# A transformer block with routed experts on one core: the setup's order of work on VectorE, and the Newton step of an inverse root

## The chip, the cores and the metric

The kernel runs on one core of a Trainium2 chip, as one program from the load of the inputs to the store of the output. The metric is device time in microseconds (us), lower is better. Three timed runs of the kernel before gave 1874.04, 1875.34 and 1876.84, a median of 1875.34.

A core has five engines that run side by side, each with its own stream of instructions in order: TensorE (PE, matrix products and transposes; the loads of its stationary operand are listed apart as PEld), VectorE (DVE), ScalarE (ACT), GpSimd (POOL) and SyncE (SP, which here issues DMAs). ACT and POOL can issue DMAs too. Engines wait for each other by semaphores.

## What is computed

The input x has 8 sequences of 1024 rows of 128 numbers, float32. Two layers are added to it: attention with relative positions, then a mixture of 8 experts with 2 chosen for each row. Cut to what matters:

```python
x = x + attn(layernorm(x), ...)          # 8 heads of 16; attn has a layernorm of its own inside
x = x + ffn(layernorm(x), ...)           # router, top 2 of 8 experts, each 128 -> 2 x 512 -> 128

# attn
xn = (inputs - mu) / sqrt(var + 1e-05) * ln_gamma + ln_beta
q, k, v = xh @ Wq + bq, xh @ Wk + bk, xh @ Wv + bv
score = (einsum(q + u_bias, k) + rel_shift(einsum(q + v_bias, p))) / sqrt(e)
ctx = softmax(score) @ v;  return ctx @ Wo + bo

# ffn: router, then sum over chosen experts of weight * (x1 * gelu(x2)) @ W2
h = gelu((h - mu) * rsqrt(var + LN_EPS) * ln_scale + ln_bias)      # h = x @ Wr1 + br1
```

Each normalization needs the inverse square root of a variance. The kernel makes it with an integer guess from the bits of the number and three Newton steps, r <- r (1.5 - 0.5 v r r).

## The kernel before

**Stages.** The program has three. A setup loads tables and weights and prepares the first sequence (batch 0) and its first group of four heads. Then a loop runs the attention of all 8 batches x 2 groups x 2 halves of the queries, with a list of side work (preparing the next batches, closing finished blocks, routing finished rows) that is placed step by step between the products. Then 71 blocks of 256 routed rows go through the experts. The router of the last two batches still runs while the first expert blocks do: `beside_experts` takes one step of it after each piece of an expert block.

**Order.** Setup and loops are written by hand: each engine gets its instructions in the order in which the program writes them. A Python generator such as `prepare` or `rsqrt` gives up control at each `yield`; the number of its `yield`s decides how its steps are spread over the loop.

**The setup's order.** Loads go first (`loads`, L1034 to L1058): on SP's queue the first batch's rows `xall` (L162), then the weights `wl` (L1039), then the tables `tb` of the first keys (L387); on ACT's queue the columns `cols` (L1040), a row of biases, and the larger tables `kl` and `ku`; POOL's queue carries small ones. Then DVE forms `vq` and adds into `cols` (L1078, L1080). `folded` (L1060) makes the weights of keys and queries: for each of two groups, PE multiplies into a bank of PSUM (L1067), DVE adds the own part into `wc` (L1068), PE multiplies two columns (L1071), DVE adds them into `bias` (L1072). The key product later uses `wc` as its stationary operand; DVE's first use of that product needs `bias`.

**`prepare(0)`** (L345) follows. DVE takes the moments of 8 tiles of 128 rows (`moments`, L235 and L236: one BATCH_NORM_STATS2 and one BATCH_NORM_AGGREGATE each), then the inverse root of 8 variances per partition (`rsqrt`, L220 to L229), then writes `xn` (L357) for 8 tiles. PE transposes `xn` in two halves (L370), ACT scales and moves each into `xT` (L371). Up to the `yield 2` after `xn` only DVE works; PE and ACT come in behind it. For later batches `prepare` runs the Newton steps and xn on POOL (`eng` is `nc.gpsimd` there).

**`keys(0, 0)`** (L381) follows: products of `xT` with `wc` (L338), four of them in two halves, each read by DVE into `z` or `kt` (L402, L405), then copies by DMA (L414 to L419), and then the first scores (L507).

**`rsqrt`** has four callers: `prepare` for batch 0 (DVE) and for the others (POOL), and the router twice per pair of batches (`route`, L659): on POOL for the first three pairs, on DVE for the last (`late`). The guess (L220, L221, L223) always runs on DVE.

**The experts.** For each block `hidden` multiplies (L1234, L1235), ACT and DVE make the gated product (L1237, L1238), `result` multiplies back (L1247). `turn_in` transposes the next block's rows, and DVE copies them into `xt` (L1224), which the next block's first product reads.

Of the kernel before, what the change touches and what calls it, by code (L numbers as in the profile page):

```python
# [45 lines left out]
ALU = mybir.AluOpType  # L46
# [3 lines left out]
P = 128  # L50
# [98 lines left out]
def kernel(ctx: ExitStack, tc: tile.TileContext, a: dict, out: bass.AP):  # L149
    nc = tc.nc  # L150
# [47 lines left out]
    def bank(name):  # L198
        return ps_ms.tile([P, QB], F32, name=name, tag="ms")
# [15 lines left out]
    def rsqrt(eng, pool, r, var, eps, use="", scale=1.0):  # L215

        n = var.shape[1]
        v = pool.tile([P, NRT], F32, name="rs_v", tag=f"rs_v{use}")[:, 0:n]
        s = pool.tile([P, NRT], F32, name="rs_s", tag=f"rs_s{use}")[:, 0:n]
        nc.vector.tensor_scalar(v, var, float(scale), float(eps), ALU.mult, ALU.add)  # L220
        nc.vector.tensor_scalar(s.bitcast(I32), v.bitcast(I32), 1, None, ALU.logical_shift_right)  # L221
        yield
        nc.vector.tensor_scalar(r.bitcast(I32), s.bitcast(I32), -1.0, 1597463007.0, ALU.mult, ALU.add)  # L223
        yield
        for _ in range(3):
            eng.tensor_tensor(s, r, r, ALU.mult)
            eng.tensor_tensor(s, s, v, ALU.mult)
            eng.tensor_scalar(s, s, -0.5, 1.5, ALU.mult, ALU.add)
            eng.tensor_tensor(r, r, s, ALU.mult)  # L229
            yield  # L230

    def moments(pool, mv, src, n):

        st = pool.tile([P, 6], F32, name=f"st_{n}", tag="bnst")
        nc.vector.bn_stats(st, src)  # L235
        nc.vector.bn_aggr(mv[:, n, :], st)  # L236

    def col(mv, k):
        return mv[:, :, k:k + 1].rearrange("p n o -> p (n o)")
# [35 lines left out]
    with ExitStack() as at:  # L275
# [44 lines left out]
        wc = [acst.tile([P, 2, P], F32, name=f"wc{g}") for g in range(NG)]  # L320
        bias = [acst.tile([P, 2], F32, name=f"bias{g}") for g in range(NG)]
# [23 lines left out]
        def prepare(b):  # L345

            sl = slice(b * NT, (b + 1) * NT)
            for n in range(b * NT, (b + 1) * NT):
                moments(rk, mv1, xall[:, n, :], n)
                yield  # L350

            eng = nc.gpsimd if b else nc.vector
            yield from rsqrt(eng, rk, r1[:, sl], col(mv1, 1)[:, sl], 1e-10, "p", 1.0 + 1e-5)
            xn = ap1.tile([P, NT, D], F32, name=f"xn{b}", tag="xn")
            if b == 0:
                for n in range(NT):
                    nc.vector.tensor_scalar(xn[:, n, :], xall[:, n, :], mv1[:, n, 0:1], r1[:, n:n + 1], ALU.subtract, ALU.mult)  # L357
            else:
                nc.gpsimd.tensor_tensor(xn, xall[:, sl, :], col(mv1, 0)[:, sl].unsqueeze(2).to_broadcast([P, NT, D]), ALU.subtract)
                nc.gpsimd.tensor_tensor(xn, xn, r1[:, sl].unsqueeze(2).to_broadcast([P, NT, D]), ALU.mult)  # L360
            if 0 < b < NB - 1:
                nc.sync.dma_start(xall[:, (b + 1) * NT:(b + 2) * NT, :], x_v[:, (b + 1) * NT:(b + 2) * NT, :])
            yield
            yield 2
            xts[b] = xt = ap1.tile([P, S], F32, name=f"xT{b}", tag="xT")
            for hf in range(NQ):
                yield 0
                pt = bank(f"xt{b}_{hf}") if b else scores(4 + hf)
                for n in range(TQ):
                    nc.tensor.transpose(pt[:, n * P:(n + 1) * P], xn[:, hf * TQ + n, :], ident)  # L370
                nc.scalar.activation(xt[:, hf * QB:(hf + 1) * QB], pt, AF.Identity, bias=gb[:, 1:2], scale=gb[:, 0:1])  # L371
                yield
            if b:
                nc.gpsimd.tensor_tensor(xall[:, sl, :], xall[:, sl, :], rows_bc[:, DR + NE:].unsqueeze(1).to_broadcast([P, NT, D]), ALU.add)
            yield
# [95 lines left out]
        def scores(k):  # L471
            return sct[k].tile([P, QB], F32, name=f"sc{k}", tag=f"sc{k}")
# [186 lines left out]
        def route(t0, late):  # L659
# [15 lines left out]
            r2 = small("r2", [nt], u)  # L675
            eng = nc.vector if late else nc.gpsimd
            yield from rsqrt(eng, rk, r2, col(mv2, 1)[:, sl], 1e-5)

            def rows(q):
# [27 lines left out]
            for i in range(n_q + 2):  # L707
                for k in range(4):
# [11 lines left out]
                    if k % 2 == 0 or i >= 2:  # L720
                        yield
            rh = small("rh", [nt], u)
            yield from rsqrt(eng, rk, rh, col(mvh, 1), 1e-6)
            lg = small("lg", [nt, NE], u)

# [305 lines left out]
        def run(gen):  # L1031
            for _ in gen:
                pass

        def loads():

            wl = app.tile([P, HG, QB], F32, name="wl", tag="px").rearrange("p j c -> p (j c)")
            wl, lt = wl[:, 0:W_C], wl[:, W_C:W_C + P]
            nc.sync.dma_start(wl, a["wl"][:, 0:W_C])  # L1039
            nc.scalar.dma_start(cols, a["wl"][:, W_C:W_END])  # L1040
            row = ap2.tile([P, S + 1], F32, name="row", tag="vt")
            row, ones = row[0:1, 0:DR + NE + D], row[0:1, QB:QB + P]
            nc.vector.memset(ones, 1.0)
            nc.scalar.dma_start(row, a["row"])
            for g in range(NG):
                nc.scalar.dma_start(kls[g][:, 0:S], a["tab_l"][g])
                nc.scalar.dma_start(kus[g], a["tab_u"][g])
            nc.scalar.dma_start(blk, a["blk"])
            nc.scalar.dma_start(wo_p, a["wo_p"])
            nc.gpsimd.dma_start(wr1_sb, a["Wr1"])  # L1050
            nc.gpsimd.dma_start(wr2_sb, a["Wr2"])
            for i, n in enumerate(("ln_scale", "ln_bias")):
                nc.gpsimd.dma_start(lns[:, i:i + 1], a[n].rearrange("(p o) -> p o", o=1))
            nc.gpsimd.dma_start(lt, a["lt"])
            nc.gpsimd.dma_start(rev, a["rev"])
            nc.gpsimd.dma_start(xs[NE * REG:NE * REG + BT, :].rearrange("(p r) x -> p (r x)", p=P), zero)
            nc.gpsimd.dma_start(ys[NPAIR:NPAIR + P, :], zero[:, 0:D])
            return wl, lt, row, ones  # L1058

        def folded(wl):  # L1060

            wqT = wl[:, 0:P]
            for g in range(NG):
                gm = wl[:, P + 4 * P * g:P + 4 * P * g + 2 * P]
                own = wl[:, P + 4 * P * g + 2 * P:P + 4 * P * g + 4 * P]
                pm = scores(2 * g)
                nc.tensor.matmul(pm[:, 0:2 * P], lhsT=wqT, rhs=gm, start=True, stop=True)  # L1067
                nc.vector.tensor_tensor(wc[g].rearrange("p k c -> p (k c)"), pm[:, 0:2 * P], own, ALU.add)  # L1068
                pc = scores(2 * g + 1)
                for k in range(2):  # L1070
                    nc.tensor.matmul(pc[:, k:k + 1], lhsT=gm[:, k * P:(k + 1) * P], rhs=vq, start=True, stop=True)  # L1071
                nc.vector.tensor_tensor(bias[g], pc[:, 0:2], padded[:, g, :], ALU.add)  # L1072

        with tc.manual_schedule():
            wl, lt, row, ones = loads()
# [2 lines left out]
            nc.vector.tensor_tensor(vq, cols[:, 5:6], cols[:, 6:7], ALU.add)  # L1078
            padded = cols[:, 7:7 + 2 * NG].rearrange("p (g k) -> p g k", k=2)
            nc.vector.tensor_tensor(padded[:, :, 0], padded[:, :, 0], cols[:, 7 + 2 * NG:7 + 3 * NG], ALU.add)  # L1080
            folded(wl)
            run(prepare(0))
            run(keys(0, 0, state[0, 0]))
            pb = bank("rows")
            nc.tensor.matmul(pb[:, 0:DR + NE + D], lhsT=ones, rhs=row, start=True, stop=True)
# [345 lines left out]
```

## Time and profile before

The profiled execution took 1875.47 us as a run; its span, from first to last instruction, is 1873.8. By stage, from windows of the profile:

| from, to (us) | PE busy | DVE busy | ACT busy | POOL busy | granted PE clock |
|---|---|---|---|---|---|
| 0 to 30 | 11.39 | 16.83 | 2.84 | 8.58 | 1.00 |
| 30 to 90 | 58.21 | 37.76 | 11.64 | 8.48 | 0.63 |
| 90 to 1440 | 1297.95 | 920.98 | 780.48 | 798.01 | 0.98 |
| 1440 to 1844 | 396.95 | 239.29 | 180.60 | 195.08 | 0.99 |
| 1844 to 1873.8 | 8.74 | 10.98 | 3.77 | 8.43 | 0.72 |

A row gives the microseconds in which each engine executed something. PE's matmuls overlap and their ends are modelled, so a busy PE is not yet a PE at its peak. The granted clock is the share of full speed that PE got, by the profile's record of changes; ahead of the first recorded change it reads 1.00. The first two rows are the setup and the fill of the attention pipeline, where the second phase of each block has not begun.

A line of the order of instructions reads: start, duration, engine, line of the program, operation, output <- inputs, shapes, count, and in brackets how long the engine had been idle and what ended that.

### The profile page before, as it was taken

The numbers are of one execution on the slowest core, as the hardware profiler recorded it, in microseconds if no ns is written. First come the engines' busy times: TensorE is split into PE (matmuls) and PEld (weight loads), VectorE is DVE, ScalarE is ACT, GpSimd is POOL, SyncE is SP. The second block draws the span as 40 slices with busy tenths as digits, with TensorE's granted clock in tenths as the row PEclk, the third lists the DMA queues.
The fourth block names the chain that finished last, engine by engine and source line by source line (L and its number), as shares of the span: only waits on it lengthen the run. The fifth ranks groups of instructions, "written<-read, shape, count | busy, mean of one in ns | idle before, by whom it ended". The sixth has DMA issues, their size and how long they took to land. (4 is left out here: it accounts for less than half of the span.)

```text
span 1873.8 us, 45516 instructions
## 1 busy us (share of the span) xinstructions
PE 1773.2 (95%) x17332; PEld 990.5 (53%) x17332; DVE 1225.8 (65%) x3274; ACT 979.3 (52%) x1922; POOL 1018.6 (54%) x1414
## 2 busy tenths in 40 slices
PE   6999999999998999999979999998988999999995
PEld 2344444444443444344434444444434988899995
DVE  5767686677677576667757687775841656655554
ACT  1265656656565555466545655664545444444442
POOL 2154353446637747854585686567582435743353
PEclk8699999999999999999989999999998999999998
DMA  5021120112102011201111221101012557766696
GB/s 158 1 48 35 33 38 27 27 30 61 27 27 39 27 27 51 58 29 27 32 34 29 60 55 37 27 28 27 18 59 59 183 169 222 224 214 203 211 338 209
DMA packets 97293, 150.35 MB, mean 80 GB/s; under 512 B 25345, under 2 KB 68610, under 8 KB 97074
## 3 DMA queue, kind: packets, MB, share of 16 engines
q1 hardware_dynamic: 78448, 122.27, 24.0%
q0 software_dynamic: 8912, 18.15, 2.7%
q10 hardware_dynamic: 9714, 7.02, 1.3%
q8 instruction: 137, 2.24, 0.5%
q14 instruction: 82, 0.67, 0.1%
HBM read 106.78 MB, written 23.55 MB: 70 GB/s over the span
## 5 line engine op out<-in xcount | busy, mean ns | idle before, releaser
L543 ACT ACTIVATE px<-sc 128x512 f32<-128x512 f32 x1152 | 632.9, 597 | 519.5 <-PE sc L507 309.5
L522 DVE CUSTOM_DVE_ANT_0 jk<-sc,wide 128x512 f32<-128x512 f32 x576 | 396.9, 689 | 146.4 <-PE sc L507 103.9
L507 PE MATMUL sc<-kl,z 32*128 32x512 f32 (+3 forms) x1536 | 401.9, 549 | 14.4 <-ACT px L543 9.5
L507 PE MATMUL sc<-ku,zu 32*128 32x128 f32 (+3 forms) x2304 | 374.7, 405 | 7.6 <-ACT px L543 7.1
L518 DVE TENSOR_REDUCE mx<-sc 128x1 f32<-128x512 f32 x448 | 287.7, 684 | 138.0 <-PE sc L507 128.7
L507 PE MATMUL sc<-zu,ku 32*128 32x512 f32 (+3 forms) x1536 | 359.9, 546 | 0.0
L593 PE MATMUL av<-px,va 128*32 128x256 f32 (+3 forms) x3792 | 350.6, 442 | 6.7 <-POOL px L555 6.1
L507 PE MATMUL sc<-z,kl 32*128 32x512 f32 (+3 forms) x1536 | 337.2, 518 | 0.1
L507 PEld LDWEIGHTS sc<-ku,zu 32*128 32x128 f32 x2304 | 198.5, 188 | 70.5 <-ACT px L543 53.7
L1264 POOL DMA_INDIRECT ys<-yo,to x142 | 137.3, 967 | 152.9 <-DVE to L1259 51.1
L507 PEld LDWEIGHTS sc<-kl,z 32*128 32x128 f32 x1536 | 141.7, 187 | 133.9 <-ACT px L543 97.7
L593 PEld LDWEIGHTS av<-px,va 128*32 128x32 f32 x3792 | 75.2, 108 | 234.6 <-issue 143.8
L1238 DVE SCALAR_TENSOR_TENSOR gt<-h,wb,gl 128x256 f32<-128x256 f32 x280 | 132.4, 482 | 92.2 <-ACT gl L1237 91.6
L1237 ACT ACTIVATE gl<-h,wb 128x256 f32<-128x256 f32 x280 | 129.6, 473 | 119.0 <-PE h L1235 117.3
L1234 PE MATMUL h<-xt,wb 128*128 128x256 f32 x560 | 169.7, 385 | 7.0 <-issue 5.6
L555 POOL TENSOR_SCALAR_AFFINE_SELECT px<-px 128x516 f32<-128x516 f32 (+1 forms) x128 | 85.0, 664 | 158.1 <-ACT px L543 157.8
L1235 PE MATMUL h<-xt,wb 128*128 128x256 f32 x560 | 168.4, 383 | 0.0
L536 PE MATMUL sc<-mT,onesb 32*128 32x512 bf16 x1152 | 164.7, 380 | 0.0
L507 PEld LDWEIGHTS sc<-z,kl 32*128 32x128 f32 x1536 | 124.6, 186 | 67.5 <-ACT px L543 29.3
L507 PEld LDWEIGHTS sc<-zu,ku 32*128 32x128 f32 x1536 | 117.6, 186 | 80.1 <-ACT px L543 37.8
L840 POOL DMA_INDIRECT xs<-rw,slot x128 | 125.7, 982 | 37.6 <-issue 35.2
L1247 PE MATMUL y<-wb,gt 128*128 128x128 f32 x1120 | 136.3, 275 | 0.0
(284 smaller groups left out, 2329.7 us busy)
## 6 DMA issues: line engine op xcount, KB each, us to landing
wb<-in_wx SPq DMA_DIRECT2D x70, 836.0 KB
tb<-in_tab SPq DMA_DIRECT2D x32, 512.0 KB
xb<-xs SPq DMA_DIRECT2D x68, 130.0 KB
yk<-ys SPq DMA_DIRECT2D x32, 256.0 KB
zu<-z SPq DMA_DIRECT2D x124, 64.0 KB
xall<-in_inputs SPq DMA_DIRECT2D x8, 512.0 KB
kl<-kt SPq DMA_DIRECT2D x64, 64.0 KB
rx<-inv SPq DMA_DIRECT2D x128, 32.0 KB
```

Source lines behind the costliest of these rows:

```text
L507: nc.tensor.matmul(ps[:, c0:c0 + w], lhsT=lhs[r, l0:l0 + P], rhs=rhs[r, r0:r0 + w], start=first, stop=final)
L518: nc.vector.tensor_reduce(to, p, AX.X, ALU.max)
L522: nc.vector.tensor_tensor_reduce(jk, p, wide[:, m0:m0 + QB], 1.0, 3.0 * BIG, ALU.add, ALU.max, to)
L536: nc.tensor.matmul(p, lhsT=onesb[r, :], rhs=mts[n][r, :], start=first, stop=not first)
L543: nc.scalar.activation(pxs[n, k][:, j, :], p, AF.Exp)
L593: nc.tensor.matmul(avs[n][32 * j:32 * j + 32, c0:c1], lhsT=va[:, kt, j].rearrange("p o d -> p (o d)"), rhs=px[:, j, c0:c1], start=(k == 0) ...
L1234: nc.tensor.matmul(ph[:, 1, :], lhsT=wb[:, FF + c * P:FF + (c + 1) * P], rhs=xt, start=True, stop=True)
L1235: nc.tensor.matmul(ph[:, 0, :], lhsT=wb[:, c * P:(c + 1) * P], rhs=xt, start=True, stop=True)
L1237: nc.scalar.activation(gl, ph[:, 1, :], AF.Gelu_apprx_tanh, bias=wb[:, B1_0 + NFC + c:B1_0 + NFC + c + 1])
L1238: nc.vector.scalar_tensor_tensor(gt[:, c, :], ph[:, 0, :], wb[:, B1_0 + c:B1_0 + c + 1], gl, ALU.add, ALU.mult)
L1247: nc.tensor.matmul(y[:, k, :], lhsT=gt[:, c, k * P:(k + 1) * P], rhs=wb[:, W2_0 + c * D:W2_0 + (c + 1) * D], start=(c == 0), stop=(c == NF ...
L1264: ins = nc.gpsimd.indirect_dma_start(ys_v[HB * i + k], bass.IndirectOffsetOnAxis(ap=to[:, k:k + 1], axis=0), yo[:, k, :], None).ins
```

## The change

Two edits. In `rsqrt`, if the engine is DVE, a Newton step has three instructions instead of four: s = (-0.5 r) r; s = s v; r = (s + 1.5) r. The `yield` after each step stays. On POOL the step is as before. Nine instructions are gone in all: three in the setup, six in the late router.

In the setup, `folded` becomes a generator: it first writes all products of PE for both groups, keeps the four additions in a list, gives up control, and writes the additions when it is resumed. The caller runs `folded` up to that point, then `prepare(0)` up to its `yield 2` (moments, root and `xn`), then the additions, then the rest of `prepare(0)`.

```diff
@@ rsqrt
         for _ in range(3):
+            if eng is nc.vector:
+                eng.scalar_tensor_tensor(s, r, -0.5, r, ALU.mult, ALU.mult)
+                eng.tensor_tensor(s, s, v, ALU.mult)
+                eng.scalar_tensor_tensor(r, s, 1.5, r, ALU.add, ALU.mult)
+                yield
+                continue
             eng.tensor_tensor(s, r, r, ALU.mult)
             eng.tensor_tensor(s, s, v, ALU.mult)
             eng.tensor_scalar(s, s, -0.5, 1.5, ALU.mult, ALU.add)
@@ folded
-            wqT = wl[:, 0:P]
+            wqT, adds = wl[:, 0:P], []
             for g in range(NG):
...
-                pm = scores(2 * g)
+                pm, pc = scores(2 * g), scores(2 * g + 1)
                 nc.tensor.matmul(pm[:, 0:2 * P], lhsT=wqT, rhs=gm, start=True, stop=True)
-                nc.vector.tensor_tensor(wc[g].rearrange("p k c -> p (k c)"), pm[:, 0:2 * P], own, ALU.add)
-                pc = scores(2 * g + 1)
                 for k in range(2):
                     nc.tensor.matmul(pc[:, k:k + 1], lhsT=gm[:, k * P:(k + 1) * P], rhs=vq, start=True, stop=True)
-                nc.vector.tensor_tensor(bias[g], pc[:, 0:2], padded[:, g, :], ALU.add)
+                adds.append((wc[g].rearrange("p k c -> p (k c)"), pm[:, 0:2 * P], own))
+                adds.append((bias[g], pc[:, 0:2], padded[:, g, :]))
+            yield
+            for to, x, y in adds:
+                nc.vector.tensor_tensor(to, x, y, ALU.add)
@@ setup
-            folded(wl)
-            run(prepare(0))
+            fold, prep = folded(wl), prepare(0)
+            next(fold)
+            while next(prep) != 2:
+                pass
+            run(fold)
+            run(prep)
             run(keys(0, 0, state[0, 0]))
```

## The prediction

> **What bounds the kernel now.** I read the page first, then the order of instructions over the first 60 us, then windows of 3.41 us with the granted clock, then the chain of waits and two short stretches of the experts. The page's first rows:
>
> ```profile
> span 1873.8 us, 45516 instructions
> PE 1773.2 (95%) x17332; PEld 990.5 (53%) x17332; DVE 1225.8 (65%) x3274; ACT 979.3 (52%) x1922; POOL 1018.6 (54%) x1414
> ```
>
> TensorE (PE) sets the end nearly everywhere: in windows cut by stage it is busy 1298.0 of 1350 us from 90 to 1440 and 397.0 of 404 from 1440 to 1844. It is not the bound ahead of 30 us, with 11.4 of 30. So an edit pays only if it brings PE's first long run forward, or takes an instruction from under a wait of PE. In the order of instructions (start, duration, engine, line, operation) the setup is one thread of waits:
>
> ```profile
> 4.96 0.16 DVE L1080 TENSOR_TENSOR cols<-cols 128x2 f32<-128x2 f32 x1
> ...
> 7.39 1.22 PE L1067 MATMUL sc<-wl 128*128 128x256 f32 x2 [7.39 <-DMA wl<-in_wl]
> ...
> 8.65 0.42 DVE L1068 TENSOR_TENSOR wc<-sc,wl 128x256 f32<-128x256 f32 x1 [3.54 <-PE sc L1067]
> ...
> 11.00 0.16 DVE L1072 TENSOR_TENSOR bias<-sc,cols 128x2 f32<-128x2 f32 x1 [0.22 <-PE sc L1071]
> 11.08 0.28 DVE L235 BATCH_NORM_STATS2 st<-xall 128x6 f32<-128x128 f32 x1
> ...
> 15.44 0.17 DVE L220 TENSOR_SCALAR rs_v<-mv 128x8 f32<-128x8 f32 x1
> ...
> 18.49 2.14 DVE L357 TENSOR_SCALAR xn<-xall,mv,r 128x128 f32<-128x128 f32 x8
> ...
> 20.17 0.78 ACT L371 ACTIVATE xT<-sc,cols 128x512 f32<-128x512 f32 x1 [9.39 <-PE sc L370]
> ...
> 21.09 5.03 PE L338 MATMUL sc<-xT,wc 128*32 128x512 f32 x32
> ```
>
> The reader is to see VectorE (DVE) free from 5.12 (4.96 + 0.16), idle 3.54 us for the weights, then held by four additions with gaps until 11.08, and only then at the moments; PE's key products wait for the end of that thread at 21.09. What follows hangs on them: kt, its copies by DMA, the first scores at 29.85.
>
> **The moved additions.** Let T be when DVE can begin the moments. DVE itself is free at 5.12, the lower bound. `wl` is queued behind `xall` on SP's queue and is used at 7.39, the upper bound. In the DMA view cut into fifths of a microsecond, packets under 2 KB number 30, 9, 8 and then 0 from 4.6 to 5.4: `xall`'s rows (512 bytes) end near 5.1. SP's queue falls from 91% to 47% of the engines at 5.8 to 6.0, where the bytes moved reach those of `xall` and `wl` together (1.1 MB), and PE uses `wl` 1.4 us later. The `cols` load was used 0.5 to 0.7 us after its last packets. So T is an estimate of 5.1 plus 0.6 to 1.4; I take 6.2.
>
> From T the moments take 15.44 - 11.08 = 4.36. The root took 18.49 - 15.44 = 3.05 for 15 instructions, 0.203 each; three fewer make 2.44. From the first xn to the first key product were 21.09 - 18.49 = 2.60 by way of PE's transposes and ACT. The product is reached at T + 4.36 + 2.44 + 2.60 = T + 9.40. The other way to it is DVE: xn takes 2.14, then wc's first addition 0.42, and with two gaps of 0.05 that is T + 9.46. The two meet, so take T + 9.5 = 15.7. Before it was 21.09: **a gain of 5.4** (6.5 at T = 5.1, 4.2 at T = 7.4), of which 0.61 is the shorter root.
>
> The other three additions cost 0.16 + 0.42 + 0.16 and gaps, about 0.9; they lie beside the first key product, of 1.96 (21.09 to z's 23.05), and DVE's first use of it comes after. Without that cover they would cost their 0.9. PE's order is unchanged: all six products of the folded weights already stand ahead of the transposes, and they ended at 10.96. Opening batch 0's `prepare` issues no DMA, so nothing moves past SP's or POOL's queue. The new wait is DVE's for `xall`: behind it stand 36 instructions, then the four additions, and PE's key product waits for those. The tables of `keys` must be there: the last bytes of SP's queue pass between 15 and 16 us; the second half is first used about 19.5, so 2 us are spare even with 1.4 for landing.
>
> **The instruction that replaces two.** The trace has the form at the same size:
>
> ```profile
> L924 DVE SCALAR_TENSOR_TENSOR endsa<-endsa,full x1: 168/168/168, 1390.1 to 1390.1; 128x8 f32<-128x8 f32 x1
> ```
>
> 168 ns, against 168 to 172 for each of the four in a step now; a step loses one pitch of 0.203.
>
> **The last batches' router.** Six more instructions go (two roots, three steps): 1.2 us of DVE. Only the first step of each root stands ahead of a copy that PE waits for:
>
> ```profile
> 1510.30 0.17 DVE L229 TENSOR_TENSOR rh<-rh,rs_s 128x16 f32<-128x16 f32 x1
> 1510.39 0.42 DVE L1224 COPY xt<-xp 128x256 f32<-128x256 f32 x1
> ...
> 1510.91 0.67 PE L1234 MATMUL h<-xt,wb 128*128 128x256 f32 x2 [0.37 <-issue]
> ```
>
> The copy ends at 1510.81 and PE starts at 1510.91, after 0.37 idle; at 1466.79 it is the same (copy to 1466.69, 0.72 idle). So 2 x 0.20 = **0.4**, bounds 0 and 1.2. The other four I cost at nothing: DVE is idle there behind PE's pairs of 0.43. Without that cover they are 0.8.
>
> **PE's clock.** This is what can spoil or swell the sum. Windows (PE, PEld, DVE, ACT, POOL busy; granted clock; DMA share; GB/s):
>
> ```profile
> 27.35:30.76 3.41, 0.91 (x2) 0.32 (x3) 0.95 (x3) 0.00 (x0) 0.00 (x0) 1.00 0.55 79
> 30.76:34.17 3.41, 3.41 (x7) 1.46 (x6) 1.77 (x5) 0.00 (x0) 1.09 (x1) 0.50 0.91 185
> ...
> 44.42:47.83 3.41, 3.33 (x18) 1.50 (x15) 3.23 (x6) 0.65 (x2) 0.00 (x0) 1.00 0.00 0
> ...
> 51.24:54.66 3.42, 2.29 (x43) 1.72 (x44) 1.22 (x4) 2.33 (x5) 0.87 (x2) 1.00 0.00 0
> 54.66:58.07 3.41, 3.41 (x20) 1.70 (x16) 1.90 (x5) 0.19 (x1) 1.58 (x3) 0.50 0.00 0
> ```
>
> The clock falls to half at 30.76, returns at 44.42, falls at 54.66 and returns at 85.38: distances of 13.66, 10.24 and 30.72, that is 4, 3 and 9 times 3.41. It fell after a window with little PE work (0.91, 2.29). A start 5.4 us earlier meets these steps at other places. One step more or less at half clock is 3.41 us at half rate, 1.7; with two falls and two returns I bound this at ±3.4 and take 0.
>
> The key products are at half rate too, though the record says 1.00: the first took 1.96, like the 1.94 of L338 at 34.82 with 0.50 granted, later ones 0.85. Before, the window 17.11 to 20.52 held 1.54 us of transposes and did not raise the rate. Afterwards the transposes and the first product share a window. If all four products stay slow, 2.2 is lost; if they turn fast a product sooner, 1.5 is won. I take 0, nearest to the row that is there.
>
> [...]
>
> **Sum.** 5.4 + 0.4 = 5.8 off the profiled execution's own 1875.47 (span 1873.8 and 1.7 around it): 1869.7. That execution lies 0.13 above the median of the runs shown, 1875.34; I say **1869.6**. Its own range, from T, the key products and the steps of the clock, is 1866 to 1873.
>
> **Rivals.** *The clock returns where it returned.* If 85.38 is a fixed place, what is won ahead of it is won at half rate: 5.4 / 2 + 0.4 = 3.1, 1872.3. For it: the half clock from 54.66 held for nine steps though PE showed 3.4 of 3.4 in many of them. Against: a return depends on the work, and that comes earlier.
>
> *Slower: one more long stretch at half clock.* If the shifted steps cut PE's work after 85 us so that one window holds as little as the 2.29 above, the clock halves for as long as it did then, 30.7 us, while PE is the bound: 15.4 lost, 1869.6 + 15.4 = 1885.0. It decides from about 19 us of added half clock; one short spell, such as the 10.2 after PE's wait near 607 us, costs 5.1 and only brings 1874.7. For it: PE waits for POOL's hT (8.5 us near 603 and 954) with half clock behind each. Against: from 90 to 600 the granted clock is 1.00 throughout.
>
> *The half clock ends sooner.* Three steps fewer from 54.66 give back 5.1: 1864.5. For it: 72 to 85 us is bound by PE at half rate, DVE falls there to 0.84 of 3.42.
>
> *The new branch is not taken.* If the test of the engine's identity fails, twelve instructions stay twelve: 0.61 and 0.4 are missing, 1870.6. Against it: the caller passes the very object that is compared.
>
> **How the numbers follow.** Forecast 0.58, clock fixed 0.17, sooner 0.13, more half clock 0.09, branch 0.03. The runs shown lie 2.8 apart; about 0.2% (3.75 us) is what they can tell from no change, so faster is below 1871.6 and slower above 1879.1. Of the forecast 0.05 lies over 1871.6: faster 0.53 + 0.13 + 0.03 = 0.69, same 0.17 + 0.05 = 0.22, slower 0.09. The range 1864.5 to 1874.5 leaves out the slower case, half of the sooner one and the edges of the others, about 2 in 10.
>
> **What would show it.** The first BATCH_NORM_STATS2 at 5.7 to 6.6 behind the `xall` load, nine Newton instructions in place of twelve with 2.4 us from L220 to xn, wc's addition straight after xn, the first key product near 15.7, kt's copies near 22 and the first score near 24.4 instead of 29.85. From 100 us on every row should lie 5.4 earlier. Wrong would be a first key product after 17, half clock beyond 85 us in sum over 45 us, or a shift that is there at 30 and gone at 100.

## The result and the profile after

The changed kernel takes 1869.18 us, median of six runs (1866.68 to 1869.41), against 1875.18 for the kernel before in six runs (1874.04 to 1876.84): a ratio of 0.9963, 95% interval 0.9951 to 0.9975. That is 6.0 us in the medians. The profiled execution took 1869.21 with a span of 1867.5, 6.3 under the span before. A second set of six runs gave 0.9969 (0.9957 to 0.9982).

The page of the changed kernel, its first two rows:

```profile
span 1867.5 us, 45508 instructions
PE 1773.6 (95%) x17332; PEld 990.5 (53%) x17332; DVE 1226.7 (66%) x3265; ACT 978.7 (52%) x1922; POOL 1019.5 (55%) x1414
```

PE is as busy as before (1773.6 against 1773.2 us) in a span that is 6.3 shorter: no work of PE went away, it only begins earlier. DVE has nine instructions fewer (3265 against 3274). The order of instructions over the setup (lines are those of the changed file; the moments are L241 there, the root L220 to L229, xn L363, the additions L1080):

```profile
4.61 0.15 DVE L1088 TENSOR_TENSOR cols<-cols 128x2 f32<-128x2 f32 x1
...
5.42 0.29 DVE L241 BATCH_NORM_STATS2 st<-xall 128x6 f32<-128x128 f32 x1 [0.65 <-DMA xall<-in_inputs]
...
6.88 1.22 PE L1073 MATMUL sc<-wl 128*128 128x256 f32 x2 [6.88 <-DMA wl<-in_wl]
...
9.78 0.17 DVE L220 TENSOR_SCALAR rs_v<-mv 128x8 f32<-128x8 f32 x1
...
12.20 2.14 DVE L363 TENSOR_SCALAR xn<-xall,mv,r 128x128 f32<-128x128 f32 x8
...
14.26 0.41 DVE L1080 TENSOR_TENSOR wc<-sc,wl 128x256 f32<-128x256 f32 x1
...
14.82 5.11 PE L344 MATMUL sc<-xT,wc 128*32 128x512 f32 x32
```

DVE now waits 0.65 for the rows, not 3.54 for the weights' products, and works through to xn. The additions, from 14.26 on, find PE's products long done (the last ended at 10.44). The first key product starts at 14.82 instead of 21.09, 6.27 earlier.

What became of these 6.27 can be followed by markers. One instruction on DVE, the maximum `most` at the end of a block's first phase (L566 before), occurs once for each of 32 blocks:

| marker | before | after | earlier by |
|---|---|---|---|
| first key product | 21.09 | 14.82 | 6.27 |
| first score | 29.85 | 23.66 | 6.19 |
| block 1, `most` | 67.8 | 61.5 | 6.3 |
| block 14 | 598.7 | 592.2 | 6.5 |
| block 32 | 1389.5 | 1383.4 | 6.1 |
| expert product behind the late router's first root | 1466.79 | 1460.52 | 6.27 |
| the one behind its second root | 1510.91 | 1504.44 | 6.47 |
| last addition of the end | 1869.27 | 1863.03 | 6.24 |

These are single executions. In them the setup's gain is passed on nearly whole through 1,400 us; the late router adds 0.4 near 1466 and 1510; 0.2 is given back at the end.

The clock took the same four steps. Before, it fell at 30.76, returned at 44.42, fell at 54.66 and returned at 85.38; afterwards the four are at 24.67, 38.32, 48.56 and 79.28, all 6.10 earlier, with 44.4 us at half clock in both up to 100 us. Windows of the changed kernel (columns as in the prediction):

```profile
21.25:24.67 3.42, 1.01 (x3) 0.49 (x4) 0.88 (x3) 0.00 (x0) 0.00 (x0) 1.00 0.59 86
24.67:28.08 3.41, 3.41 (x7) 1.14 (x5) 1.83 (x5) 0.00 (x0) 1.09 (x1) 0.50 0.86 179
...
45.15:48.56 3.41, 2.28 (x41) 1.79 (x42) 1.08 (x4) 2.31 (x5) 0.99 (x2) 1.00 0.00 0
48.56:51.97 3.41, 3.41 (x19) 1.47 (x12) 2.10 (x6) 0.07 (x1) 1.45 (x3) 0.50 0.00 0
```

The windows ahead of the falls hold 1.01 and 2.28 of PE, where they held 0.91 and 2.29 before: the same pieces of work.

### The profile page after: what moved, and what is told of

Its sections match the earlier page's. It is cut to its first block, busy times and chain, and to the rows that moved or that the text cites. A ratio compares the mean times of both kernels' runs of the same rounds, so it can differ in the third digit from the quotient of the medians.

```text
span 1867.5 us, 45508 instructions
## 1 busy us (share of the span) xinstructions
PE 1773.6 (95%) x17332; PEld 990.5 (53%) x17332; DVE 1226.7 (66%) x3265; ACT 978.7 (52%) x1922; POOL 1019.5 (55%) x1414
```

## The experiments

There are nine experiments: eight kernels, and the changed kernel a second time. The first four and the last two ran on a chip on which every kernel is some 55 us slower; the kernel before takes 1930.06 there (35 runs). Their times are therefore read as ratios to it, and the places in their traces by the distance from the start. Up to block 14 their traces run like those of the first chip (block 14 in the run with the order alone: 593.8, 14 blocks after a first key product at 15.62); the longer waits come from about 690 us on, in all six traces from there. Why that chip has them is not shown. The last two were executed once each, for their traces; their times (1926.11 and 1921.04, the kernel before 1932.77 beside them) are single values, and nothing is read from them.

**The order alone**: the four-instruction step everywhere, the new order kept.

```diff
-            if eng is nc.vector:
-                eng.scalar_tensor_tensor(s, r, -0.5, r, ALU.mult, ALU.mult)
...
-                continue
```

> The changed kernel with the Newton step of four instructions everywhere; only the order of the setup is the new one. Theory A (one thread on VectorE, passed on 1:1): the root of the setup is 0.61 longer again, so the first key product starts near 15.4 instead of 14.8, the late router loses its 0.4 again; time near 1870.2, that is 5.0 under before. Theory B (the gain is a lucky cut of the clock's steps, and the setup has slack): no fixed relation, anywhere from 1867 to 1875.

Measured: ratio 0.9977 (0.9963 to 0.9990), 4.4 under before, 1.9 to 7.1 by the interval. Moments start at 5.59, first key product at 15.62, 10.03 later; before it was 21.09 - 11.08 = 10.01. Block 1's marker is at 62.3, 0.8 behind that of the changed kernel (61.5), just as the first key product is (15.62 - 14.82). In the profiled execution the clock took steps of the same lengths as in the kernel before (13.7, 10.2 and 30.7), so theory B's lucky cut is not needed to explain that its blocks come earlier. Most of the gain is the order's.

**The Newton step alone**: the kernel before with the new branch in `rsqrt`.

> The kernel before with the Newton step of three instructions on VectorE; the order of the setup is the old one. Theory A: moments start at 11.1 as before, first key product near 20.5 instead of 21.1, and 0.4 more in the experts; time near 1874.2, that is 1.0 under before. Theory B: no fixed relation. A third view, that the shorter root is the larger part of the gain, would give 1871 or less.

Measured: ratio 0.9990 (0.9978 to 1.0003), medians 1.2 apart, not clear of nothing by the times alone. The trace shows what the step does in the setup: moments at 10.64, first key product at 20.02, 9.38 later instead of 10.01. So the root is 0.63 shorter, and the third view, that the root is the larger part, falls. That the moments begin at 10.64 and not 11.08 is the weights' load, which PE used at 6.95 in that execution, not at 7.39. At the first key product this execution is 1.07 ahead of the kernel before, at block 14 only 0.34 (598.37 against 598.71); its clock took other steps, as a table below shows. So the shorter root is shown, and what it brings at the end is not, beyond the 1.2 of the medians.

**The setup delayed again.**

```diff
             next(fold)
+            idle = rk.tile([P, 6], F32, name="idle", tag="idle")
+            for _ in range(20):
+                nc.vector.bn_stats(idle, xall[:, 0, :])
             while next(prep) != 2:
```

> The changed kernel with 20 idle BATCH_NORM_STATS2 of 128 numbers on VectorE ahead of the moments, about 0.3 each, 6.1 together. Theory A (passed on 1:1): first key product near 20.9, time near 1875.3, as before. Slack behind the setup: the start moves by 6.1 and the end by less, time under 1873.

Measured: ratio 1.0001 (0.9990 to 1.0012): the whole gain is gone. The 20 idle instructions took 6.5, not 6.1; the first key product is at 21.50, which is 0.41 behind the kernel before, and the late router gives 0.4 back. By the times, time in the setup is passed on 1:1 within an interval of about 2 us. The profiled execution alone shows less: its block 14 is at 597.1, 4.9 behind the changed kernel and not 6.7. Its first stretch at half clock was 6.8 long instead of 13.7; the section on the prediction comes back to this.

**The weights' load first.**

```diff
-    nc.sync.dma_start(xall[:, 0:NT, :], x_v[:, 0:NT, :])
...
             nc.sync.dma_start(wl, a["wl"][:, 0:W_C])
+            nc.sync.dma_start(xall[:, 0:NT, :], x_v[:, 0:NT, :])
```

> The changed kernel with the load of the weights ahead of the load of the first rows on SP's queue. Theory A (the moments start when the rows land, T): 0.59 MB more ahead of them at some 0.4 MB per us, T near 6.9 instead of 5.4, first key product near 16.3, time near 1870.7. Rival (T is when VectorE itself is free, or cols): T stays at 5.4, time 1869.2.

Measured: ratio 0.9983 (0.9974 to 0.9992), 3.3 under before. The start of the moments and the first key product:

```profile
8.04 0.29 DVE L240 BATCH_NORM_STATS2 st<-xall 128x6 f32<-128x128 f32 x1 [2.75 <-DMA xall<-in_inputs]
...
17.45 1.08 PE L343 MATMUL sc<-xT,wc 128*32 128x512 f32 x4
```

DVE waits 2.75 for the rows: T is their landing, and the rival (T set by DVE or by `cols`, which was used at 5.06 here) falls. The rows landed later than expected, 8.04 instead of 6.9; why is not shown. (The 0.4 MB per us of the expectation is what the kernel before shows: 364 to 461 GB/s in the fifths of a microsecond from 4.6 to 6.2.) But 17.45 - 8.04 = 9.41, the distance that the prediction gave.

**The changed kernel again** stood as a control beside the next two, on a chip where the kernel before takes 1875.25.

> The changed kernel itself again, beside the next two on one chip. Theory A: ratio to the kernel before near 0.9967 (6 under 1875 or 1930).

Measured: 1869.59, ratio 0.9969 (0.9957 to 0.9982).

**PE's gap filled**, to see what the clock is worth.

```diff
+            warm = ps_av.tile([P, QB], F32, name="warm", tag="av")
+            for _ in range(3):
+                nc.tensor.matmul(warm, lhsT=ident, rhs=xts[0][:, 0:QB], start=True, stop=True)
             nc.scalar.copy(rows_bc, pb[:, 0:DR + NE + D])
```

> The changed kernel with three products of 512 columns (ident with xT, into the bank of the later av, read by nobody) on PE behind the row product, about 2.6 us of PE in the 3.2 us in which PE waits for the copies of kt. Theory C (the clock falls near 24.7 because that window holds little PE work, and the half clock is worth time): no fall near 24.7, the first block's marker (most, L566 in the kernel before, 61.5 in the changed kernel) about 2 to 4 earlier, and the end with it. Rival D (the fill of the pipeline is paced by VectorE and DMA, the clock does not matter there): the fall is gone or not, and the marker stays within 0.5 of 61.5.

Measured: 1869.15, ratio 0.9969 (0.9956 to 0.9981), nothing won. The first fall came at 27.37 instead of 24.08 in the control, one step later; but the clock returned the second time at 81.99 and not 78.70, and the sum at half clock is 44.4 as in the control. Block 1's marker is at 61.7 (control 61.3), block 2's at 107.1 (105.4). Theory C is wrong in its size, in that the fall would stay away, and in the reason that it gives for the fall. The two windows ahead of the fall:

```profile
20.54:23.95 3.41, 3.00 (x8) 1.05 (x6) 1.25 (x4) 0.00 (x0) 0.00 (x0) 1.00 0.44 59
23.95:27.37 3.42, 3.41 (x8) 0.88 (x6) 2.10 (x6) 0.00 (x0) 0.92 (x1) 1.00 0.94 188
```

They held 3.00 and 3.41 us of PE by the record, and the clock fell all the same. So little recorded PE work in the window ahead, which the prediction too names for the falls and on which its slower rival rests, is not a condition of a fall; what brings one is not shown. The later fall also won nothing at its own place: the next products of the values (`pv`) waited until 28.80 for ACT's copy `rows_bc`, which waited for a DMA, with PE idle for 1.40; in the control they start at 28.29.

**The fill kept busy as well.**

```diff
+                    if half == 1 and t < LAG_B:
+                        nc.tensor.matmul(warm, lhsT=ident, rhs=xts[0][:, 0:QB], start=True, stop=True)
                     aside(2 * t + half, half == 0)
```

> As the run with the filled gap, with one more such product on PE after each of the first 11 units of the loop. Theory C: the second fall near 48.6 is gone as well, half clock under 20 us up to 120 us instead of 44.4, and the marker of the second block (105.7 in the changed kernel) 5 or more earlier. Rival D: the products only cost PE their time, and the marker of the second block is as before or later by up to 5.

Measured: 1866.59 (1865.70 to 1871.60), ratio 0.9961 (0.9949 to 0.9973); its interval overlaps the control's, so whether it beats the changed kernel is not clear. Five of its eight runs lie at 1865.7 to 1866.7, three at 1871.0 to 1871.6. Windows between its clock steps, then those of the control:

```profile
28.49:31.91 3.42, 3.42 (x13) 0.71 (x14) 0.23 (x3) 0.87 (x2) 2.36 (x1) 0.50 0.85 228
31.91:62.63 30.72, 28.92 (x168) 11.43 (x162) 22.50 (x55) 4.76 (x11) 3.60 (x9) 1.00 0.09 31
62.63:72.87 10.24, 10.24 (x38) 3.19 (x38) 4.38 (x9) 0.91 (x2) 1.34 (x3) 0.50 0.00 0
```

```profile
24.08:37.74 13.66, 13.66 (x39) 3.42 (x38) 5.38 (x13) 1.70 (x3) 3.45 (x2) 0.50 0.67 178
37.74:47.98 10.24, 9.03 (x78) 4.33 (x78) 7.58 (x16) 3.66 (x9) 0.79 (x2) 1.00 0.00 0
47.98:78.70 30.72, 30.14 (x116) 12.23 (x118) 21.17 (x55) 4.12 (x8) 4.26 (x11) 0.50 0.00 1
```

Half clock is 13.7 us in sum instead of 44.4, under the 20 of theory C. A second fall still came, at 62.63, and it lasted 10.2 instead of 30.7. The marker of block 2 is at 104.1, against 105.4 in the control, 1.3 earlier; theory C said 5 or more, rival D as before or later. But the added products themselves took 13.0 us of PE between 28.5 and that marker. 30.7 us less of half clock are worth at most 15.4, an estimate from the 0.50 granted in these windows, and 15.4 - 13.0 = 2.4. So this run does not tell what the clock is worth in the fill, nor whether DVE or PE sets the pace there.

**The additions ahead of xn.**

```diff
-            while next(prep) != 2:
-                pass
+            for _ in range(13):
+                next(prep)
             run(fold)
```

> The changed kernel with the four additions between the root and xn instead of behind xn. Theory A (they are hidden only behind xn, where ACT works on xT beside them): they delay xn by their 0.9, and the first key product comes at T + 10.3 instead of T + 9.4, T the start of the moments. Rival (their place does not matter once they are out of the way of the moments): T + 9.4.

Measured in the order of instructions:

```profile
5.47 0.29 DVE L241 BATCH_NORM_STATS2 st<-xall 128x6 f32<-128x128 f32 x1 [0.66 <-DMA xall<-in_inputs]
...
12.15 0.42 DVE L1080 TENSOR_TENSOR wc<-sc,wl 128x256 f32<-128x256 f32 x1
...
12.95 2.13 DVE L363 TENSOR_SCALAR xn<-xall,mv,r 128x128 f32<-128x128 f32 x8
...
15.55 5.06 PE L344 MATMUL sc<-xT,wc 128*32 128x512 f32 x32
```

The first key product comes at T + 10.08, against T + 9.40: the four additions, 0.80 from 12.15 to 12.95, cost 0.7 where nothing covers them. Behind xn they cost nothing: in the changed kernel they run from 14.26 to 15.14, beside ACT's two moves of xT (13.88 to 14.66 and 14.91 to 15.69), and PE's weight load for the first key product waits 0.22 for the first of these. Of the change's gain 0.7 is thus the place behind xn, not only the place behind the moments.

**The late router with the old step.**

```diff
-            if eng is nc.vector:
+            if eng is nc.vector and use == "p":
```

> The changed kernel with the Newton step of four instructions in the late router alone; the setup keeps three. Theory A (one instruction less in the first step of each root stands ahead of the copy xt that PE waits for): first key product at T + 9.4 as in the changed kernel, and PE's idle times at the two places in the experts back at 0.72 and 0.37 as before, 0.2 longer each than in the changed kernel. Rival (the late router's instructions are hidden throughout): the two idle times as in the changed kernel.

Measured: moments at 5.58, first key product at 15.00, 9.42 later. At the second place in the experts, the changed kernel first, then this one:

```profile
1503.92 0.42 DVE L1236 COPY xt<-xp 128x256 f32<-128x256 f32 x1
...
1504.44 0.67 PE L1246 MATMUL h<-xt,wb 128*128 128x256 f32 x2 [0.16 <-issue]
```

```profile
1528.56 0.42 DVE L1236 COPY xt<-xp 128x256 f32<-128x256 f32 x1
...
1529.07 0.67 PE L1246 MATMUL h<-xt,wb 128*128 128x256 f32 x2 [0.37 <-issue]
```

PE idles 0.37 with four instructions ahead of the copy, 0.16 with three; the kernel before had 0.37. At the first place the old step gives 0.99, and the run with the additions ahead of xn, which has the new step, 0.78 on the same chip (0.72 before and 0.53 after on the first chip). So 0.19 to 0.21 at each place, on both chips; the rival, that the router's instructions are hidden throughout, falls for these two. The second place is the firmer one: over all traces it has 0.16 or 0.17 with the new step (eight) and 0.37 or 0.38 with the old (three). The first has one exception, 0.97 with the new step in the run with the Newton step alone; DVE was there one instruction less far in the guess of that root than in the other traces of that chip.

## Why the prediction was right

It said 1869.6, from 5.8 off the profiled execution; that came out at 6.3, and the median is 1869.18. Step by step:

- **T**, the start of the moments, was mis-sized: 6.2 was taken, 5.42 came (5.42 to 5.63 in all eight profiles with the new order and the rows' load first), so its sign, moments at 5.7 to 6.6, was missed on the early side. The rows' small packets end near 5.0 in the changed kernel (28, 6 and 0 under 2 KB in the fifths from 4.6 to 5.2), so the load was used about 0.4 after them; the estimate had 0.6 to 1.4, of which the upper figure came from the weights' load. The lower bound, 5.1, was the better guess.
- **The distance from T to the first key product** was given as 9.40 by way of xn's transposes and 9.46 by way of the additions. It measured 9.38 to 9.42 in the eight traces with the new step and the additions not ahead of xn, and 10.01 and 10.03 with the old step. Its pieces: moments 4.36 (4.36 said), root 2.42 (2.44), from xn to the product 2.62 (2.60).
- **The additions' cover** was priced at 0.9 for the three that lie beside the key product. The run that moves all four ahead of xn shows 0.7 for the four, so the price was somewhat high.
- **The key products** were entered at 0, with 2.2 lost or 1.5 won as bounds. All of them together took 5.11, against 5.03 before; in the nine other traces 4.38 to 5.63.
- **The replacing instruction** was taken as dear as those it replaces, by a row of the same size; the shorter root, 0.63 by the run with the Newton step alone, bears that out (0.61 said).
- **The late router's 0.4** came as about 0.2 at each of the two places named.
- **No slack behind the setup** was assumed. The delayed kernel gives the gain back whole by its median, and the table below shows 1:1 where the clock takes the same steps.
- **The clock** was entered at 0 with ±3.4. In the profiled execution it was 0: the same four steps, 6.10 earlier. *The clock returns where it returned* falls with that: 85.38 became 79.28. What the prediction holds against it, that a return depends on the work, agrees with the run with the fill kept busy: with the added products the second return came 10.2 behind its fall, against 30.7 in the control. The stretch that the slower rival needed did not come either, and the return did not come sooner in that execution. The branch was taken: the trace shows nine Newton instructions in the setup. That the clock's share came out at 0 is in part luck: two of the other eight profiles without products added on PE drew another cut of the steps that is worth about 2 us. One sign of being wrong could not tell anything: read as the half clock after 85 us, it is 76.8 in sum, far over the 45 named, but it was 77.3 in the kernel before.

The gain of 5.8 was thus right by its mechanism, with 0.9 more ahead of the first key product, most of it from T, and 0.4 lost on the way to the end.

**What the clock's steps do.** The prediction bounded them by half of every microsecond at half clock. The nine traces without products added on PE show when a start is passed on whole. Here are the start of the first key product, how far behind it the clock first falls, how long that first half-clock stretch is, and how far behind the same product the markers of blocks 1 and 14 come (us):

| trace | first key product | first fall behind it | stretch | block 1 behind it | block 14 behind it |
|---|---|---|---|---|---|
| Newton step alone | 20.02 | 8.4 | 17.1 | 46.2 | 578.4 |
| late router old | 15.00 | 9.0 | 13.7 | 46.6 | 577.0 |
| changed, control | 14.84 | 9.2 | 13.7 | 46.5 | 577.1 |
| before | 21.09 | 9.7 | 13.7 | 46.7 | 577.6 |
| additions ahead of xn | 15.55 | 9.7 | 13.7 | 46.6 | 577.4 |
| changed | 14.82 | 9.8 | 13.7 | 46.7 | 577.4 |
| order alone | 15.62 | 10.3 | 13.7 | 46.7 | 578.2 |
| delayed | 21.50 | 10.7 | 6.8 | 44.1 | 575.6 |
| weights first | 17.45 | 10.9 | 6.8 | 44.6 | 575.3 |

In the six with a first stretch of 13.7 block 1 comes 46.5 to 46.7 behind the first key product, whether that starts at 14.8 or at 21.1: the start is passed on 1:1. At block 14 these six still lie within 1.2 of each other. In the two traces in which the first fall comes 10.7 and 10.9 behind the product, the stretch is 6.8, two steps shorter, and the rest follows about 2 us sooner (block 1 at 44.1 and 44.6). Half clock is 37.5 us in sum there instead of 44.4. The windows of the run with the weights first:

```profile
24.92:28.33 3.41, 1.80 (x4) 0.58 (x4) 0.64 (x2) 0.00 (x0) 0.00 (x0) 1.00 0.80 132
28.33:35.16 6.83, 6.83 (x19) 1.70 (x18) 2.24 (x9) 1.01 (x2) 3.45 (x2) 0.50 0.83 200
35.16:48.81 13.65, 12.32 (x95) 5.13 (x96) 10.07 (x20) 4.39 (x10) 0.83 (x2) 1.00 0.17 60
```

Its first half-clock stretch is 6.83 long, not 13.65. Its first key product is 17.45 - 14.82 = 2.63 behind that of the changed kernel, its block 1 (62.1 against 61.5) only 0.6: 2.0 won. In the delayed kernel it is 21.50 - 14.82 = 6.68 and 65.6 - 61.5 = 4.1, so 2.6 won. Two steps less at this place are worth 2.0 to 2.6, where half of 6.83 would be 3.4; one step less at the first fall brought nothing in the run with the filled gap, where PE waited for other engines. So here the half was a bound, as the prediction had it, and not a price.

Such a draw is likely behind some of the lower runs too. Two steps less raise the mean granted clock by half of 6.83 in 1867, which is about 0.002, and the two lower runs of the changed kernel, 1866.68 and 1867.37, have 0.970 against 0.968 in the other four. Of the fifteen executions of the kernel before beside the control, the five with 0.970 are the five shortest (1873.05 to 1874.32). It is not all: the control's two shortest, 1867.84 and 1868.14, have 0.968 like its others but one.

## What to carry to other kernels

In an engine's in-order stream, look for an instruction that waits for a late load ahead of work whose data are already there; swapping them is worth the wait, but also look for the place further down where the moved instruction lies beside other engines' work, which was 0.7 of the gain here. A gain at the start of a program bound by one engine reaches its end whole if nothing behind the setup has slack (here 6.27 at the first key product, 6.24 at the last addition). A deliberate delay of the same size tests that by the median of several runs; one trace alone can mislead, because the clock's steps need not lie at the same places of the work: in two executions of the changed kernel they lay 0.58 to 0.59 apart, and the first key product 0.02. An experiment that adds work to the bounding engine has to count that work: here 13.0 us of added products hid what the clock gave. Of the instructions saved in the late router on DVE, 66% busy here, only those counted that stand directly ahead of something that the bounding engine waits for: two of six, 0.2 each.

## What was not expected of the hardware

The clock's steps lay whole multiples of 3.41 us apart (13.65, 10.24 and 30.72 in both profiled executions), but not at fixed places of the program: between the two all four steps moved by 6.10, which is not a multiple of 3.41, while the work moved by 6.2 to 6.3. Between the changed kernel and its control, the same program, the four steps moved by 0.58 to 0.59, and the first key product by 0.02. The clock stayed at half for 30.7 us, nine times 3.41, while the record shows PE busy for 30.14 of 30.72 (the control's 47.98 to 78.70), and it fell behind a window with 3.41 of 3.41 in the run with the filled gap. PE time by the record thus neither brought the clock back here nor held it, and what does is not shown.

Two chips differed by 55 us with the same program (the kernel before takes 1930.06 on one and 1875.25 on the other), from about 690 us on. At block 14 they did not yet: it comes 575.3 to 578.4 behind the first key product on the slower chip, 577.1 to 577.6 in the three traces of the table that are not from it. So each run here is set against the kernel before on its own chip, and not against a time of another.
